# ScalarE's pieces of a second-layer norm queued two bank reads behind their scales, in a fused scan and Hadamard-FFN kernel

## Chip, cores and metric

One core of a Trainium2 chip runs the whole program. The metric is the device time in microseconds (us); lower is better. Float32 throughout.

## What is computed

The input x has 4 images of 512 rows by 512 channels. Two layers are applied, each as `x = x + layernorm(f(layernorm(x)))`. Cut to what matters:

```python
# layer 1: gated scan                      # layer 2: FFN, width 2048
i, f, g = h @ Wi.T, h @ Wf.T, h @ Wg.T     hidden = silu(h @ W1.T) * (h @ W3.T)
gate = sigmoid(f); v = silu(i)*(1-gate)    hidden = fwht(hidden)
o = scan over rows of (gate, v)            out = hidden @ W2.T
o = rms_norm(o) * gnorm * g * sigmoid(g)
out = o @ Wo
```

The Walsh-Hadamard transform (fwht) is folded into W2 once, early in the program.

## The kernel before, in words

**Products.** Every matrix product is split in the Winograd way into seven products of half-size blocks, P1, P2, P6, P5, P7, P3, P4 in this order (`ORDER`, L33; `seven`, L444). A set of seven uses three PSUM banks, X, Y and Z. X takes P1, P6, P7 and P4 one after the other, Y takes P2, Z takes P5 and P3. After each product the bank is read: P1, P6, P5 and P4 are copied out by ScalarE (L470), P2, P7 and P3 are added to a quarter of the result by VectorE (L468). The next product into the same bank has to wait for that read: P6 waits for the copy of P1, P4 for the read of P7. In these texts a "read" means one of the three VectorE reads.

**Units.** An attention unit `attn_unit(b, u)` (L511) is one set for image b: u=0 and u=1 give two halves of the scan, u=2 the output gate. `ffn_unit(b, m)` (L621) is one of eight sets of the first FFN matrices. `attn_out(b)` (L572) is the set for Wo, `ffn_out` (L637) one for W2; these are not run in one go, but put into the queue `fill`. `run` (L112) goes through the seven products k = 0..6 of a unit, and after each of them may take one step from `fill` (`slot`), so the sets of two stages alternate on TensorE. Units (1,0), (1,1), (2,0) and (2,1) are "dense": a slot after every product. The tile names in the profile are X_a, Y_a, Z_a for attention units, X_y, Y_y, Z_y for Wo, X_f for W1 and W3, X_po for W2.

**Small work.** The norm behind Wo and the norm in front of the FFN are cut in pieces that wait in two queues:
- `sums`: VectorE pieces. At each read of a set, `pace[what]` of them are taken (L473-L476): statistics of a quarter, `half` (two row tiles' mean and root), two `residual`s, and `scales` (L606), which issues statistics, a power on GpSimd (`rs`, L244) and the bias `nb` (L274) of the second layer's norm for two of the four row tiles.
- `acts`: ScalarE pieces. After product k of a unit, `pieces[k]` of them are taken (L117-L119), each ordered behind the latest copy of a bank (`behind("copy")`). Dense units take one after k = 0, 2, 3, 5, 6, others one after k = 0 and two after k = 3. The pieces of `scales` are the writes of `xn_f` (L289), which need `nb`. Behind the second piece of a pair follows GpSimd's store of the pair to DRAM, `xnd_f` (L298).

**Fold.** The FFN's input is the transpose of `xn_f`. `load_fold` (L401) reads it back from DRAM with eight DMAs on SyncE's queue, four for each half of the rows; `transpose_fold` (L423) has two steps of four VectorE transposes, one for each half, and a step of four block sums (T1 to T4, L152-L155). The first halves feed the FFN's first two products, the sums the third. For image 0 the load stands in `fold_beside` (L936), which `beside` calls after product k = 2 of unit (2,1). The transposes stand behind reads of units (2,1) and (2,2) (`transpose_beside`, L905). Right behind this load on SyncE's queue stand the first FFN weights, `load_ffn_w(0, 0)` (L943).

**Order.** TensorE and SyncE run in program order. For VectorE, ScalarE and GpSimd a planner orders the instructions when the program is built, by priority (program order, less an offset: 400 for bank reads, `URGENT`) and by its own estimate of when each is ready, and keeps the `behind` edges. On the chip every engine goes through its own list in that order.

The image whose second norm is made beside unit (2,0) is image 0; the Wo set in `fill` at that time belongs to image 1.

Of the kernel before, what the change touches and what calls it, by code (L numbers as in the profile page):

```python
# [44 lines left out]
def kernel(  # L45
# [42 lines left out]
    def bank(name):  # L88
        return psum.tile([P, 2, H], F32, tag="ps", name=name)
# [11 lines left out]

    beside = {}
    acts = deque()
    sums = deque()
    pace = {}
    FULL, SLOW, NONE = (
# [59 lines left out]
    def again(key, b, pool=stream):  # L166
        t = stream_tile(key, b, pool)
        nc.sync.dma_start(out=t, in_=saved[key])
        return t
# [150 lines left out]
    class OutputNorm:  # L320
# [7 lines left out]
        def quarter(self, i, j, tiles=(0, 1)):  # L328
            for t in tiles:
                nc.vector.bn_stats(  # L330
                    self.st[:, 2 * i + t, j, :], self.y[:, i, t, ts(j, H)]
                )
# [111 lines left out]
    def seven(name, multiply, quarter, done=None, add=False, by_tile=False):  # L444

        ps = {}

        def make(what, a, bb, which, first):
            if first:
                ps[which] = bank(f"{which}_{name}")
            multiply(ps[which], a, bb, first)
            split = by_tile and what == "P4"
            q = {"P1": (0, 0), "P5": (1, 1), "P6": (0, 1), "P2": (0, 0), "P7": (1, 1),
                 "P3": (0, 1), "P4": (1, 0)}[what]  # L460
            to = quarter(*q)
            with tc.high_priority(offset=URGENT):
                if split:
                    for t in range(2):
                        nc.vector.tensor_add(to[:, t], ps[which][:, t], to[:, t])
                        done(*q, t)
                elif what in ("P2", "P7", "P3") or add:
                    read[what] = nc.vector.tensor_add(to, ps[which], to)  # L468
                else:
                    read["copy"] = nc.scalar.copy(to, ps[which])  # L470
            if what in ("P2", "P7", "P3", "P4") and done is not None and not split:
                done(*q)
            if what in ("P2", "P7", "P3") and not by_tile:  # L473
                for _ in range(min(pace[what], len(sums))):
                    with tc.issue_after(read[what].ins):
                        sums.popleft()()  # L476

        return [partial(make, *step) for step in ORDER]

    def project(ws, xt, name, after, dense=False):  # L480
# [91 lines left out]
    def attn_out(b):  # L572

        y = {}  # L580
        w = wo_t[0] if b < 3 else [again(("wo", c), b, stream2) for c in range(2)]

        def multiply(ps, a, bb, first):
            og = ogs[b]
            if not y:
                y[0] = work.tile([P, 2, 2, D], F32, tag="wide", name=f"y_{b}", bufs=3)
            for t in range(2):
                for c in range(2):
                    nc.tensor.matmul(  # L589
                        ps[:, t, :], og[:, a, c, ts(t, P)], w[c][:, bb, :],  # L590
                        start=first and t == 0 and c == 0, stop=c == 1,
                        skip_group_check=True,
                    )

        def done(i, j):
            with tc.high_priority(offset=SOON):
                if (i, j) == (0, 0):
                    y[1] = OutputNorm(b, y[0], ves, "y")
                sums.append(partial(y[1].quarter, i, j))

                def norm(residual, t):
                    sums.append(residual)
                    if t == 0:
                        return

                    def scales():  # L606
                        apply = normalize_tiles(b, "f", 2 * i, 2, True)
                        acts.extend(partial(apply, range(t, t + 1)) for t in range(2))

                    sums.append(scales)  # L610

                if j == 1 - i:
                    sums.append(partial(y[1].half, i, norm))

        steps = seven(f"y_{b}", multiply, lambda i, j: y[0][:, i, :, ts(j, H)], done)
        return steps[:4] + [partial(squares, b)] + steps[4:]
# [255 lines left out]
    with behind("P3"):  # L872
        with tc.high_priority(offset=URGENT):
            combine_weights(2)
        with tc.high_priority(offset=SOON):
            apply = [normalize_tiles(1, "a", i, 2, True) for i in (0, 2)]
# [60 lines left out]
        load_fold(0, "f", "ht")  # L937
        transpose_beside(0, "f", ((6, "P3"), (7, "P2"), (8, "P7")))

    beside.setdefault(2, []).append(fold_beside)  # L940
    pace.update(FULL)
    attn_unit(2, 1, True)
    load_ffn_w(0, 0)  # L943
# [107 lines left out]
```

## Time and profile before

| | |
|---|---|
| median of 3 runs | 819.52 us (818.16 to 820.74) |
| the profiled execution's own time | 819.54 us |
| its span, first to last instruction | 817.4 us |
| around the span | 2.1 us |
| mean granted TensorE clock | 0.994 |
| TensorE busy | 803.8 us, 98% |
| VectorE busy | 492.8 us, 60% |
| ScalarE busy | 265.3 us, 32% |
| GpSimd busy | 67.0 us, 8% |

A timeline row gives the start, the duration, the engine, the line, the operation with output and inputs, how many instructions are merged, and in brackets the idle time ahead of it and what ended that. "PEld" is TensorE's weight load, "SPq" SyncE's DMA issue. A matmul of 256 columns shows 379 ns but follows the one before it every 216 ns, so a product of eight takes 1.73 us.

### The profile page before, as it was taken

The page shows a single profiled execution, that of the slowest core. Times are in us where ns is not written, and L with a number is a line of the kernel's source. Part 1 is how long each engine was busy: PE and PEld are TensorE (multiplying, and loading weights), DVE is VectorE, ACT ScalarE, POOL GpSimd, SP SyncE. Part 2 cuts the span into 40 slices and gives each one's busy share as a digit, 9 for nine tenths or more (in the row PEclk, how much of TensorE's full clock was granted, in tenths as well). Part 3 has the DMA queues.
Part 4 walks back from the last instruction along what each step waited for, and adds up shares of the span by engine and source line. Part 5 has one row for each costly group of instructions (what it writes and reads, how often), then busy time and mean ns, then how long its engine had stood idle before and what let it go on. Part 6 is the DMA issues. An engine that isn't in the chain of part 4 may idle for free.

```text
span 817.4 us, 9848 instructions
## 1 busy us (share of the span) xinstructions
PE 803.8 (98%) x3704; PEld 698.6 (85%) x3704; DVE 492.8 (60%) x1002; ACT 265.3 (32%) x376; POOL 67.0 (8%) x105
## 2 busy tenths in 40 slices
PE   9999998999999999999999999999999999999995
PEld 6778887888888888888888888888888888888884
DVE  6988598799777874454335458635543534544345
ACT  4554645444343122122411223323332111331111
POOL 2120102112111010010100000101000000100000
PEclk9999999999999999999999999999999999999998
DMA  9995355666867873544654354726383442544201
GB/s 327 401 351 219 113 220 183 197 238 209 311 245 285 300 277 145 208 162 164 254 157 191 121 163 157 294 91 226 117 254 130 187 180 91 204 156 188 88 4 51
DMA packets 66415, 160.62 MB, mean 196 GB/s; under 512 B 4800, under 2 KB 40256, under 8 KB 66368
## 3 DMA queue, kind: packets, MB, share of 16 engines
q1 hardware_dynamic: 57168, 115.69, 40.6%
q0 software_dynamic: 8480, 43.00, 13.3%
q10 hardware_dynamic: 720, 1.31, 0.4%
q8 instruction: 29, 0.48, 0.2%
q14 instruction: 18, 0.15, 0.1%
HBM read 115.94 MB, written 44.04 MB: 196 GB/s over the span
## 4 chain that ended last, share of the span: by engine, by line
PE 89%; DVE 6%; DMA 2%; issue 1%; POOL 0%; ACT 0%; POOLq 0%; DVEq 0%; SPq 0%
PE X_f L487 26%; PE X_po L647 13%; PE Z_f L487 13%; PE X_a L487 7%; PE Z_po L647 7%; PE Y_f L487 7%; PE X_y L589 3%; PE Y_po L647 3%; PE Z_a L487 3%; PE Y_a L487 2%; DMA wg<-in_Wg_dram 2%; PE Z_y L589 2%; PE h L744 1%; DVE o L523 1%; PE Y_y L589 1%
## 5 line engine op out<-in xcount | busy, mean ns | idle before, releaser
L487 PE MATMUL X_f<-xt_f,w 128*128 128x256 f32 x1024 | 242.1, 379 | 0.1
L487 PEld LDWEIGHTS X_f<-xt_f,w 128*128 128x128 f32 x1024 | 194.1, 190 | 27.3 <-DVE d_f L468 0.5
L470 ACT COPY d_f<-X_f 128x512 f32<-128x512 f32 x96 | 56.1, 585 | 329.8 <-PE X_f L487 289.5
L647 PE MATMUL X_po<-w,ht 128*128 128x256 f32 x512 | 120.9, 379 | 0.2 <-DVE f L468 0.2
L487 PE MATMUL Z_f<-xt_f,w 128*128 128x256 f32 x512 | 120.9, 379 | 0.0
L647 PEld LDWEIGHTS X_po<-w,ht 128*128 128x128 f32 x512 | 97.2, 190 | 13.8 <-DVE f L468 0.6
L487 PEld LDWEIGHTS Z_f<-xt_f,w 128*128 128x128 f32 x512 | 97.3, 190 | 13.2
L468 DVE TENSOR_TENSOR f<-X_po,f 128x512 f32<-128x512 f32 x51 | 35.1, 688 | 93.9 <-PE X_po L647 93.9
L502 DVE TENSOR_TENSOR ht<-d_f 128x1024 f32<-128x1024 f32 x32 | 39.1, 1222 | 60.2 <-ACT d_f L623 45.4
L647 PE MATMUL Z_po<-w,ht 128*128 128x256 f32 x256 | 60.5, 379 | 0.0
L487 PE MATMUL Y_f<-xt_f,w 128*128 128x256 f32 x256 | 60.5, 379 | 0.0
L647 PEld LDWEIGHTS Z_po<-w,ht 128*128 128x128 f32 x256 | 48.6, 190 | 6.6
L487 PEld LDWEIGHTS Y_f<-xt_f,w 128*128 128x128 f32 x256 | 48.6, 190 | 6.6
L468 DVE TENSOR_TENSOR d_f<-X_f,d_f 128x512 f32<-128x512 f32 x32 | 22.1, 690 | 50.7 <-PE X_f L487 43.0
L244 POOL TENSOR_TENSOR rs_f<-rs_f,power 128x2 f32<-128x2 f32 x16 | 13.4, 840 | 406.4 <-DVE nm_f L345 347.1
L470 ACT COPY d_a<-X_a 128x512 f32<-128x512 f32 x36 | 21.0, 583 | 66.7 <-PE X_a L487 66.5
L623 ACT ACTIVATE d_f<-d_f 128x1024 f32<-128x1024 f32 x32 | 33.8, 1057 | 1.0
L487 PE MATMUL X_a<-xt_a,wi 128*128 128x256 f32 x128 | 33.8, 385 | 0.1
L589 PE MATMUL X_y<-wo,og 128*128 128x256 f32 x128 | 31.7, 392 | 2.2 <-ACT y L470 2.2
L487 PE MATMUL X_a<-xt_a,wf 128*128 128x256 f32 x128 | 32.8, 379 | 0.0
L468 DVE TENSOR_TENSOR d_f<-Z_f,d_f 128x512 f32<-128x512 f32 x32 | 21.9, 685 | 16.7 <-PE Z_f L487 16.7
L468 DVE TENSOR_TENSOR f<-Z_po,f 128x512 f32<-128x512 f32 x28 | 19.3, 688 | 20.2 <-PE Z_po L647 20.2
(161 smaller groups left out, 1017.3 us busy)
## 6 DMA issues: line engine op xcount, KB each, us to landing
w<-s_w SPq DMA_DIRECT2D x72, 896.0 KB, 6.2
s_w<-w POOLq DMA_DIRECT2D x24, 896.0 KB, 6.6
w<-in_W_dram SPq DMA_DIRECT2D x32, 256.0 KB, 5.4
wi<-s_wi SPq DMA_DIRECT2D x6, 896.0 KB, 8.4
wf<-s_wf SPq DMA_DIRECT2D x6, 896.0 KB, 7.9
wg<-s_wg SPq DMA_DIRECT2D x6, 896.0 KB, 5.8
w_h<-w2p POOLq DMA_DIRECT2D x8, 512.0 KB, 5.8
xnd_f<-xn_f POOLq DMA_DIRECT2D x8, 512.0 KB, 4.1
```

What stands on the lines that cost most here:

```text
L244: read["power"] = nc.gpsimd.tensor_tensor(r, r, power_t[:, 0:n], ALU.pow)
L468: read[what] = nc.vector.tensor_add(to, ps[which], to)
L470: read["copy"] = nc.scalar.copy(to, ps[which])
L487: nc.tensor.matmul(ps[:, n, :], w[:, a, c, :], xt[:, bb, c, :], start=first and n == 0 and c == 0, stop=c == 1, skip_group_check=True,)
L502: nc.vector.tensor_mul(to.rearrange("p (t k) f -> p k t f", t=2), a.rearrange("p k (t f) -> p k t f", t=2), b2.rearrange("p k (t f) -> p k ...
L523: nc.vector.tensor_tensor_scan(os_[b][:, u, h, :], gate[:, h, :], v[:, h, :], 0.0, ALU.mult, ALU.add)
L589: nc.tensor.matmul(ps[:, t, :], og[:, a, c, ts(t, P)], w[c][:, bb, :], start=first and t == 0 and c == 0, stop=c == 1, skip_group_check=True,)
L623: nc.scalar.activation(d[:, 0], d[:, 0], AF.Silu)
L647: nc.tensor.matmul(ps[:, t, :], hts[b, m][:, a, ts(t, P)], w[m][:, W2[bb], :], start=first and t == 0 and m == ms[0], stop=m == ms[-1], sk ...
L744: nc.tensor.matmul(p, h_sb, t[:, k, :], start=True, stop=True)
```

## The change

ScalarE's pieces of `scales` go into a new queue `scaled` with a count of 1 in place of `acts`. At each read, pieces with count 0 are moved to `acts`, and then the counts of those that are left go down by one; so a piece is moved at the second read after its `scales`. The load of image 0's fold is called after product k = 4 of unit (2,1) in place of k = 2.

```diff
+    scaled = deque()
...
             if what in ("P2", "P7", "P3") and not by_tile:
+                while scaled and scaled[0][0] == 0:
+                    acts.append(scaled.popleft()[1])
+                for entry in scaled:
+                    entry[0] -= 1
                 for _ in range(min(pace[what], len(sums))):
                     with tc.issue_after(read[what].ins):
                         sums.popleft()()
...
                     def scales():
                         apply = normalize_tiles(b, "f", 2 * i, 2, True)
-                        acts.extend(partial(apply, range(t, t + 1)) for t in range(2))
+                        scaled.extend([1, partial(apply, range(t, t + 1))] for t in range(2))
...
-    beside.setdefault(2, []).append(fold_beside)
+    beside.setdefault(4, []).append(fold_beside)
     pace.update(FULL)
     attn_unit(2, 1, True)
```

## The prediction, made before the change was run

> **What bounds the kernel now.** I read the page's engine shares first, then who TensorE waits for, then the timelines of TensorE, ScalarE and VectorE around the one wait of any size, then the granted clock there.
>
> ```profile
> PE 803.8 (98%) x3704; PEld 698.6 (85%) x3704; DVE 492.8 (60%) x1002; ACT 265.3 (32%) x376; POOL 67.0 (8%) x105
> PE X_y L589 <- ACT y L470: 2.2, 1, 2.2
> ```
>
> TensorE is busy for 98% of the span, and in the waits view its longest wait by far is a single one: a product of the Wo set waits for ScalarE's copy of its bank. Elsewhere I compared the starts of products with 216 ns for each matmul: behind the first 12 us no other place loses more than 0.33 us. So a change to ScalarE's or VectorE's order can gain what this one place costs, and no more. The place, on TensorE and then on ScalarE:
>
> ```profile
> 123.83 1.03 PE L487 MATMUL Z_a<-xt_a,wf 128*128 128x256 f32 x4
> 127.05 3.32 PE L589 MATMUL X_y<-wo,og 128*128 128x256 f32 x8 [2.19 <-ACT y L470]
> 130.16 1.43 PE L487 MATMUL X_a<-xt_a,wi 128*128 128x256 f32 x4
> 131.43 1.03 PE L487 MATMUL X_a<-xt_a,wf 128*128 128x256 f32 x4
> ```
>
> ```profile
> 118.47 1.06 ACT L546 ACTIVATE o<-o 128x1024 f32<-128x1024 f32 x1
> 125.22 1.31 ACT L289 ACTIVATE xn_f<-x,nb_f,rs_f 128x512 f32<-128x512 f32 x1 [5.69 <-DVE nb_f L274]
> 126.44 0.56 ACT L470 COPY y<-X_y 128x512 f32<-128x512 f32 x1
> ```
>
> ScalarE stands idle for 5.69 us at a piece of xn_f whose bias is not there. The copy of X_y behind it had its data since 119.5 (the product began at 117.79), and TensorE's P6 into that bank needs it. The bias is late because VectorE has no gap from 117 to 124.4:
>
> ```profile
> 123.70 0.75 DVE L349 SCALAR_TENSOR_TENSOR x<-y,rs_y,x 128x512 f32<-128x512 f32 x1
> 125.02 0.16 DVE L274 SCALAR_TENSOR_TENSOR nb_f<-mv_f,rs_f 128x2 f32<-128x2 f32 x1 [0.58 <-POOL rs_f L244]
> ```
>
> **What the place costs.** P6 was due at 123.83 + 4 x 0.216 = 124.69 and began at 127.05: 2.36 us. Its eight matmuls took 130.16 - 127.05 = 3.11 us from start to start, not 1.73: 1.38 more. The next four took 1.27, not 0.86: 0.41 more. Sum 4.15 us. The second and third terms are a lowered clock:
>
> ```profile
> 117.00:124.70 7.70, 7.70 (x37) 6.58 (x35) 7.44 (x14) 1.54 (x2) 0.77 (x1) 1.00 0.00 0
> 127.00:130.40 3.40, 3.35 (x9) 2.75 (x10) 3.37 (x6) 1.23 (x1) 2.19 (x3) 0.58 0.50 204
> ```
>
> The granted clock (third from the right) is 1.00 before and 0.58 after the wait. A wait of 2.4 us here thus costs up to 1.8 us of slow matmuls on top.
>
> The Trainium skill ("TensorE: Matmul & The Clock Gate", section "HAM oscillation — how this bites in real kernels") has idle gaps of more than about 3.4 us as what lowers the clock. This gap is shorter and the clock fell, so the row decides; by the page's rule the slow stretch would not be the wait's doing, and 2.36 us would be all there is to gain.
>
> **Part 1, the pieces.** I counted the queues by hand. Image 0's first scales come at P3 of unit (1,2). Before, the first xn_f piece was taken after k = 2 of unit (2,0), ahead of P1 of Wo, and the others after k = 5, k = 6 and k = 0 of unit (2,1). With the change the first pair passes P2 of (2,0) and enters acts at its P7; the pieces are taken after k = 5 and k = 6. The second scales (P3 of (2,0)) are unmoved; that pair enters acts at P7 of Wo and is taken after k = 2 and k = 3 of (2,1). No instruction is added or removed.
>
> At k = 5 the latest copy is that of X_y's P1, so the edge itself puts that copy ahead of the first piece. The copy then runs at about 119.6 to 120.2, and P6 starts when due. Removed: 4.15 us. The piece still waits for nb_f at 125.0 and ends at 126.5; the next copy in the queue, of P6, is ready at 126.4, and no product needs it before Wo's P7, some 8 us later. So the wait stays and nothing hurries behind it: cost 0, covered by 8 us of other products.
>
> **Part 2, VectorE loses slack.** With TensorE 4.15 us earlier, VectorE must do the same work sooner. It is busy for 17.24 of the 20 us from 125 to 145 and then idle 3.25 us until P7 of (2,1) at 149.00, about 6.0 us idle in all; 4.15 of it goes, 1.9 stays. A price against that: GpSimd's power for the second bias may now stand behind the store of the first pair, which comes after k = 6 (about 132.8, against 128.5 before), so that nb_f's second is up to 1.6 us later, and VectorE idles for it. 0.3 us remain. Between 0 and 0.5 us, I take 0. One residual of 0.72 us leaves the stretch before the FFN and a later one takes its load on; up to P7 of the FFN's second unit the count of pieces is as before.
>
> **Part 3, the fold.** No SyncE issue lies between the two places, so its order is unchanged; its time is not. Before:
>
> ```profile
> 138.24 1.34 ACT L289 ACTIVATE xn_f<-x,nb_f,rs_f 128x512 f32<-128x512 f32 x1
> 139.87 0.74 POOL L298 DMA_DIRECT2D xnd_f<-xn_f  x1 [7.07 <-ACT xn_f L289]
> 143.37 2.02 SPq L418 DMA_DIRECT2D fold_f<-xnd_f  x4
> 145.48 1.42 SPq L180 DMA_DIRECT2D w<-in_W_dram  x2
> 151.51 1.21 SPq L180 DMA_DIRECT2D w<-in_W_dram  x2
> ```
>
> The last piece now stands behind the copy of (2,1)'s P5, 145.48 before, so 141.3 to 141.9; the piece ends at 143.2, the store goes out at 143.5, and with its 3.4 us the second half's loads start at 147.0, 3.6 later than before. The last of four is issued at 148.4 and lands 4.8 us later (its row before) at 153.2. The two weight loads behind follow at 149.1; the other pair had waited for a buffer until 151.51 and now goes out at 150.5 (the buffer is free at 147.4), landing after 3.2 to 5.5 us, at 157.2 at worst. The FFN's first product, 164.27 before, is due at 160.1: 2.9 us to spare.
>
> The transposes of that half are tighter:
>
> ```profile
> 156.78 1.41 DVE L436 STREAM_TRANSPOSE xt_f<-fold_f 128x256 f32<-128x256 f32 x4
> 158.12 1.18 DVE L523 TENSOR_TENSOR_SCAN o<-d_a 128x512 f32<-128x512 f32 x1
> 161.09 0.69 DVE L468 TENSOR_TENSOR d_a<-X_a,d_a 128x512 f32<-128x512 f32 x1 [1.79 <-PE X_a L487]
> ```
>
> They would start at 152.6 and wait until 153.2 on VectorE's queue, with a scan and the P7 read of (2,2) behind them. The 1.79 us idle ahead of that read take the 0.6; cost 0. Without that cover each us of a later load goes to the read, and 0.8 us further on to TensorE at P4.
>
> **Sum.** 4.15 removed, 0 added: the profiled execution's 819.54 (span 817.4 and 2.1 around it) becomes 815.4. The median of the runs is 819.52, the same. With 0.5 us of Part 2 it is 815.9; the runs before lie within 1.3 us of their median, so 814.3 to 816.6 for this case.
>
> **Rivals.**
>
> *A smaller wait comes in its place (0.14).* VectorE, with 0.3 to 1.9 us to spare near 145, reads a bank late, or the planner, given other arrivals, puts another piece ahead of a copy. For: P7 of the FFN's first unit already starts late, because a square stands ahead of its copy on ScalarE. Against: from 150 on no wait beyond 0.5 us shows. Price 0.5 to 2.4 us with up to 1.8 of clock: 816.6 to 819.
>
> *The slow clock stays (0.03).* If it did not come from the wait, only 2.36 us go: 817.2. Against: it begins right behind the wait, and the windows around it have 1.00.
>
> *Nothing is gained (0.05).* Another instruction that needs late work is put ahead of the same copy: 819.5. The edge excludes the piece itself.
>
> *Slower: the store of the second pair lands late (0.12).* The eight stores xnd_f landed in 3.2 to 8.4 us, median 4.1. At 8.4 us the loads start at 152.0, the last lands at 158.2, the transposes end at 159.6, the scan at 160.8 and the read at 161.4, while P4 of (2,2) is due at 158.4: 3.0 us of wait and 1.7 of slow clock, 4.7 in all, or 820.1. It begins to cost at a landing of 5.4 us; past 10 us the time is above 822. Against: this pair's own stores took 3.3 and 3.4, the second with VectorE busy for 6.51 of 7 us.
>
> The Trainium skill ("SBUF — State Buffer", the "DVE blocks DMA" trap) says that DMAs issued from GpSimd's queue can be held up by VectorE's work, and gives 620 ns growing to about 3100 ns; that would speak for this rival, but the landing of 3.4 us beside a busy VectorE shows no such growth here.
>
> **Numbers.** Forecast 815.4, chance 0.66. The range 814.3 to 818.9 leaves out the last two rivals' 0.17 and a little at the low end. A difference under 0.3% (2.5 us) can't be told from none here. Faster by more means below 817.1: 0.66, half of the first rival and some of the clock's, 0.75. Slower by more means above 822.0: the worse part of the last rival, with unseen reorderings, 0.09. Same: 0.16.
>
> **What would show it.** Right: no wait of X_y on ScalarE's y in TensorE's waits; the copy of Wo's P1 near 119.6 and an xn_f piece behind it near 125; granted clock 1.00 from 124 to 131; the FFN's first product near 160.1; the second half's fold loads near 147. Wrong: a wait of X_a, X_y or X_f above 0.5 us between 125 and 200, SyncE's fold loads past 148.2, or a slow clock without a wait.

## The result, and the profile after

| | before | after |
|---|---|---|
| median of 5 runs each | 818.16 us (817.44 to 820.74) | 814.73 us (814.56 to 815.22) |
| ratio of after to before | | 0.9948, 95% interval 0.9935 to 0.9961 |
| profiled execution, its time | 819.54 us | 815.02 us |
| its span | 817.4 us | 813.2 us |
| mean granted clock | 0.994 | 0.997 |

The kernel is faster by 0.5%. The two spans differ by 4.2 us: one wait went, with the slow matmuls behind it. The two times differ by 4.5 us, because the time around the span is shorter as well, 1.8 us where it was 2.1. The page's shares, and all of TensorE's waits that are left:

```profile
PE 801.8 (99%) x3704; PEld 698.4 (86%) x3704; DVE 492.6 (61%) x1002; ACT 265.3 (33%) x376; POOL 67.5 (8%) x105
```

```profile
PE warm L825 <- POOL ident masks.py:199: 1.4, 1, 1.4
PE X_po L652 <- DVE f L469: 0.2, 1, 0.2
```

X_y no longer stands in this view. The same place in the timelines of TensorE and of ScalarE:

```profile
123.78 1.03 PE L492 MATMUL Z_a<-xt_a,wf 128*128 128x256 f32 x4
124.64 1.89 PE L594 MATMUL X_y<-wo,og 128*128 128x256 f32 x8
126.37 1.03 PE L492 MATMUL X_a<-xt_a,wi 128*128 128x256 f32 x4
```

```profile
119.66 0.59 ACT L471 COPY y<-X_y 128x512 f32<-128x512 f32 x1 [1.14 <-PE X_y L594]
125.16 1.34 ACT L290 ACTIVATE xn_f<-x,nb_f,rs_f 128x512 f32<-128x512 f32 x1 [4.91 <-DVE nb_f L275]
126.57 0.59 ACT L471 COPY y<-X_y 128x512 f32<-128x512 f32 x1
```

ScalarE still idles for 4.91 us until the bias is there. But the copy of Wo's P1 is now in front of that idle time, and P6 begins 0.86 us after the start of the four matmuls before it (4 x 0.216), with no gap. The granted clock (third from the right) is whole where it had been 0.58:

```profile
127.00:130.40 3.40, 3.40 (x17) 2.99 (x16) 3.40 (x9) 2.26 (x4) 1.46 (x3) 1.00 0.55 124
```

Behind the fold nothing is late. The second half's loads on SyncE's queue, the transposes of that half on VectorE with the read behind them, and the FFN's first product:

```profile
146.52 1.78 SPq L419 DMA_DIRECT2D fold_f<-xnd_f  x4
153.45 1.42 DVE L437 STREAM_TRANSPOSE xt_f<-fold_f 128x256 f32<-128x256 f32 x4
156.89 0.69 DVE L469 TENSOR_TENSOR d_a<-X_a,d_a 128x512 f32<-128x512 f32 x1 [0.63 <-PE X_a L492]
160.07 1.89 PE L492 MATMUL X_f<-xt_f,w 128*128 128x256 f32 x8
```

VectorE is still idle for 0.63 us ahead of the P7 read of unit (2,2), where it had 1.79.

### The profile page after: what moved, and what is told of

It is laid out like the page before. It is cut to its first block, busy times and chain, and to the rows that moved or that the text cites. A ratio compares the mean times of both kernels' runs of the same rounds, so it can differ in the third digit from the quotient of the medians.

```text
span 813.2 us, 9847 instructions
## 1 busy us (share of the span) xinstructions
PE 801.8 (99%) x3704; PEld 698.4 (86%) x3704; DVE 492.6 (61%) x1002; ACT 265.3 (33%) x376; POOL 67.5 (8%) x105
## 4 chain that ended last, share of the span: by engine, by line
PE 92%; DVE 4%; DMA 2%; issue 1%; POOL 0%; ACT 0%; POOLq 0%; DVEq 0%; SPq 0%
PE X_f L492 27%; PE X_po L652 13%; PE Z_f L492 13%; PE X_a L492 8%; PE Z_po L652 7%; PE Y_f L492 7%; PE Z_a L492 4%; PE X_y L594 3%; PE Y_po L652 3%; PE Y_a L492 2%; DMA wg<-in_Wg_dram 2%; PE Z_y L594 2%; PE h L749 1%; PE Y_y L594 1%; PE warm L825 1%
## 5 line engine op out<-in xcount | busy, mean ns | idle before, releaser
L492 PEld LDWEIGHTS X_a<-xt_a,wi 128*128 128x128 f32 x128 | 23.9, 190 | 7.7 <-issue 2.9
```

The costliest lines, as they stand in the source:

```text
L492: nc.tensor.matmul(ps[:, n, :], w[:, a, c, :], xt[:, bb, c, :], start=first and n == 0 and c == 0, stop=c == 1, skip_group_check=True,)
```

## The experiments

The theory: the whole gain is the first piece of image 0's first pair no longer standing ahead of one copy, and its size is the wait plus, in some executions, a stretch of slow clock behind it (granted clock 0.5 in place of 1.00). The rivals: the gain is spread over all pieces; it comes from the fold's place; any delay of the pieces does; the slow clock is not the wait's doing. The ratios are to the kernel before on the same chip.

**1. Which pieces, and is it the fold?** Two kernels, made from the kernel after, each hold back a part of the pieces.

```diff
-                        scaled.extend([1, partial(apply, range(t, t + 1))] for t in range(2))
+                        late = (b, i) == (0, 0)        # the other kernel: != (0, 0)
+                        for t in range(2):
+                            piece = partial(apply, range(t, t + 1))
+                            scaled.append([1, piece]) if late else acts.append(piece)
...
-    beside.setdefault(4, []).append(fold_beside)
+    beside.setdefault(2, []).append(fold_beside)       # the other kernel: 4
```

> Only the first pair of pieces of image 0 is held back two reads; all others enter acts at once and the fold's load stays at k = 2. Theory: the whole gain is the first pair's, so the time is that of the kernel after, 814.7 (within 1 us), with no wait of X_y and the clock at 1.00 there. Rival, the gain is spread over the 16 pieces or belongs to the fold's later load: about 818 or in between, 816 to 817.5.

Measured: 815.26 us (6 runs, 815.07 to 816.12), ratio 0.9956 (0.9942 to 0.997), no wait of X_y, clock 0.996 or 0.997 in every run.

> The other way round: all pairs but the first are held back two reads, and the fold's load stands at k = 4. Theory: the wait of 2.4 us at P6 of Wo is back and with it the time of the kernel before, 817.4 to 820.7. Rival (spread, or the fold): 814.7 to 816.

Measured: 818.40 us (12 runs, 816.93 to 819.98), ratio 0.9998 (0.9987 to 1.0009), and the wait is there:

```profile
PE X_y L594 <- ACT y L471: 2.2, 1, 2.2
```

So one pair of eight carries the gain. The other seven, and the fold's later load, are worth nothing that these runs can tell; the load only had to follow the second pair's store, and with the first pair alone it can stay where it was.

**2. Is any delay enough?** One read in place of two:

```diff
-                        scaled.extend([1, partial(apply, range(t, t + 1))] for t in range(2))
+                        scaled.extend([0, partial(apply, range(t, t + 1))] for t in range(2))
```

> All pairs held back one read in place of two, the load at k = 4. The first piece then enters behind the copy of P5 of unit (2,0), one product ahead of the copy of Wo's P1. Theory: what counts is the edge to that copy, which is not there, so the planner puts the piece ahead of it again: the wait of 2.4 us is back, 817.4 to 820.7. Rival: any delay of the pieces brings the gain: 814.7 to 816.

Measured: 818.37 us (12 runs, 816.79 to 821.03), ratio 0.9994 (0.9982 to 1.0006). ScalarE's timeline has the old order, the piece and then the copy:

```profile
125.42 1.31 ACT L290 ACTIVATE xn_f<-x,nb_f,rs_f 128x512 f32<-128x512 f32 x1 [6.64 <-DVE nb_f L275]
126.63 0.57 ACT L471 COPY y<-X_y 128x512 f32<-128x512 f32 x1
```

The delay as such does nothing: without an edge to the copy of Wo's P1 the planner still puts the piece first. That it takes the bias to be ready earlier than it is would explain this; no run shows the planner's estimates. Two reads is the least count that brings the edge.

**3. Is it the late bias?** The kernel before, its queues untouched, with the first scales' steps put ahead on VectorE:

```diff
-                        apply = normalize_tiles(b, "f", 2 * i, 2, True)
+                        with tc.high_priority(offset=URGENT if (b, i) == (0, 0) else 0):
+                            apply = normalize_tiles(b, "f", 2 * i, 2, True)
```

> The kernel before, with only the VectorE and GpSimd steps of image 0's first scales put ahead by priority (400), so that the bias is there near 118 and not at 125; no queue is changed. Theory: the wait came from the late bias alone; the copy of Wo's P1 then runs by 121.7, P6 starts when due, and the time is that of the kernel after, 814.7 to 815.7, unless the statistics now make a block sum or the gate late (up to 0.5 us). Rival: the place of the pieces in the queue costs by itself, or VectorE's steps in front push the gate's products back so far that TensorE waits for them: 817 to 820.

Measured: 815.33 us (6 runs, 814.85 to 816.47), ratio 0.9955 (0.994 to 0.9971). The bias on VectorE, the piece and the copy on ScalarE:

```profile
118.33 0.16 DVE L274 SCALAR_TENSOR_TENSOR nb_f<-mv_f,rs_f 128x2 f32<-128x2 f32 x1 [0.58 <-POOL rs_f L244]
118.53 1.36 ACT L289 ACTIVATE xn_f<-x,nb_f,rs_f 128x512 f32<-128x512 f32 x1 [1.08 <-DVE nb_f L274]
121.20 0.58 ACT L470 COPY y<-X_y 128x512 f32<-128x512 f32 x1
```

The piece is still ahead of the copy, and harmless, because ScalarE waits 1.08 us and not 5.69. So there are two cures of the same value: bring the late input forward, or put the waiting piece behind what is urgent. Both together:

> The kernel after with the early bias of the run with the early bias added. Theory: there is nothing left to gain at this place, so it is the same as the kernel after within 0.5 us. Rival: the bias, early, lets ScalarE run its pieces sooner and the store with them, which gives 0.5 us or more.

Measured: 815.21 us (6 runs), beside 815.14 for the kernel after in the same session (ratios 0.996 and 0.9959). Nothing more is to be had here, and no kernel tried is clearly better than the one after.

**4. Does the slow clock come from the wait?** First both kernels again, run by run.

> The kernel before, unchanged, timed run by run with its granted clock. Theory: the wait of 2.36 us at P6 of Wo is in every run, and the slow clock behind it costs between 0 and 1.8 us (or twice that) by how the wait falls in the clock's own rhythm; then the times spread over 817.2 to 821 and go with the mean granted clock, about 0.002 of clock for each 1.7 us, while the kernel after, without a wait, stays within 0.7 us. Rival: the spread of the kernel before comes from DMA or from start-up; then the clock is the same in its fast and its slow runs.

Measured: 818.17 us (12 runs), ratio to the other runs of the same kernel 0.9992 (0.998 to 1.0005). The eight runs with a mean clock of 0.996 took 817.05 to 818.71, the four with 0.994 took 819.04 to 820.81. In the sessions of the experiments the kernel before ran 84 times: 39 runs at 0.996 or above with a median of 817.75, 45 below with 819.51; over all 84 it is 819.0. The profile of this run is one without a slow stretch, at the same wait:

```profile
127.93 1.99 PE L589 MATMUL X_y<-wo,og 128*128 128x256 f32 x8 [2.19 <-ACT y L470]
129.76 1.03 PE L487 MATMUL X_a<-xt_a,wi 128*128 128x256 f32 x4
```

The eight matmuls took 1.83 us from start to start here, and 3.11 in the profile of before.

> The kernel after, unchanged, beside the kernel before on one chip. Theory: no run has a slow window (0.996 to 0.997 in all), and the median is 814.7 to 815.4; the kernel before has one in about half of its runs (41 of 73 so far), near 819.5 with and 817.8 without. Rival: the kernel after has the two kinds of runs as well, and its first five runs only missed the slower kind.

Measured: 815.14 us (6 runs, 814.6 to 815.79), ratio 0.9959 (0.9944 to 0.9974). All eleven runs of the kernel after are at 0.996 or 0.997.

Then waits of other lengths, made in the kernel after by small instructions that only occupy ScalarE. They copy a table, which nothing reads any more, onto itself.

```diff
+                elif name == "y_1" and what == "P1":
+                    with behind("copy"):
+                        for _ in range(29):            # 39, 20 and 23 in the others
+                            last = nc.scalar.activation(h_sb, h_sb, AF.Identity)
+                    with tc.issue_after(last.ins):
+                        read["copy"] = nc.scalar.copy(to, ps[which])
```

> The kernel after, with 29 small ScalarE instructions (128x128, about 0.23 us each) put ahead of the copy of Wo's P1, so that P6 waits about 1.2 us (0.5 to 2). Theory: the clock falls only when more than about 2 us of idle time lie in one of its 3.4 us windows; a wait of 1.2 us then costs itself alone, the clock stays at 0.996 to 0.997 in every run, and the time is 815.9 (815.2 to 816.7). Rival: any wait lowers the clock in some of the runs: then some of them show 0.994 or 0.995 and 817.6.

> The same with 39 such instructions, for a wait of about 3.4 us (2.7 to 4.2). Theory: nearly every run (some 85%) then has a slow window, so the median is 814.7 + 3.4 + 1.7 = 819.8 (818.5 to 821.5) with the granted clock at 0.994 to 0.995. Rival: the slow clock comes by chance whatever the length of the wait; then no more of the runs than of the kernel before, about half, show it, and the median is nearer to 818.

Both were sized wrong: one instruction took 0.34 us and not 0.23, so the waits were 4.2 and 7.6 us. On ScalarE and on TensorE, with 29 of them:

```profile
119.08 9.87 ACT L473 ACTIVATE had<-had 128x128 f32<-128x128 f32 x29
129.48 3.78 PE L600 MATMUL X_y<-wo,og 128*128 128x256 f32 x8 [4.01 <-ACT y L475]
```

Measured: 822.04 (6 runs) with clocks of 0.992 to 0.994, and 824.54 (6 runs) with 0.990 to 0.993: a slow stretch in every run. With the right size:

> The kernel after with 20 small ScalarE instructions ahead of the copy of Wo's P1; one took 0.34 us in the two probes before, so P6 waits about 1.3 us (20 x 0.34 - 5.5). Theory (the clock falls when about 2 us or more of one 3.4 us window are idle): no run with a slow window, 0.996 to 0.997 throughout, and 814.7 + 1.3 = 816.0 (815.4 to 816.8). Rival: any wait may lower the clock; then some runs show 0.994 or 0.995 and 817.7.

Measured: 816.77 (7 runs, 815.69 to 817.35), all at 0.996 or 0.997; the wait was 1.1 us. That is 0.9 us more than 814.73 + 1.1. In the profiled run P1 of Wo already begins at 118.42, not at 117.74 as in the kernel after, and another wait stands ahead of it, at 58.69:

```profile
PE X_a L498 <- DVE d_a L469: 0.8, 1, 0.8
```

This early wait comes and goes with the same program: the first profile of the kernel before has none, the second one of 0.4 us.

> The same with 23, so that P6 waits about 2.4 us, as in the kernel before, but with the norm's pieces where the change puts them. Theory: this alone gives the time of the kernel before back, 817.2 in the runs without a slow window and 818.9 in those with one, each some half of the runs (27 of 42 had one in the kernel before). Rival: part of the difference comes from the norm's order elsewhere; then 815.5 to 816.5.

Measured: 817.83 (12 runs), ratio 0.9984 (0.9975 to 0.9993); the wait was 2.1 us. Four runs at 0.993 or 0.994 took 818.27 to 818.78, the other eight (one at 0.995, the rest at 0.996 or above) 816.72 to 818.37. So a bare wait at this place, with the norm's pieces where the change puts them, brings back both kinds of runs. Their medians, 816.96 and 818.6, lie 0.8 to 0.9 below those of the kernel before over all sessions (817.75 and 819.51); 0.24 of that is the shorter wait and 0.35 the time around the span (1.77 us here, 2.12 there). The rest, some 0.2 to 0.3, is not explained and too small for these medians to show: against the kernel before in the same session (818.4 and 819.3) the medians lie 1.5 and 0.7 below.

The profiles add up more closely than the medians. From the start of P1 of Wo to the end of the span, less the wait at P6, it is 695.5 us in the kernel after and 695.6 in each of the four full-clock profiles with a wait there (20 and 23 small instructions, second profile of before, all pairs but the first).

Where the trace's record of the clock has a slow stretch, it is 3.41 us long or a multiple of it (3.41 before, 6.83 and 10.24 in the two long waits), and its edges fit a grid of 3.41 us that runs from the first change of clock on. Here is the one of before, by windows of that length:

```profile
124.14:127.55 3.41, 1.22 (x6) 0.76 (x5) 2.79 (x6) 2.33 (x3) 1.12 (x2) 1.00 0.00 0
127.55:130.96 3.41, 3.41 (x9) 2.72 (x9) 3.41 (x8) 1.23 (x2) 1.92 (x3) 0.50 0.66 271
130.96:134.37 3.41, 3.41 (x17) 2.98 (x16) 2.02 (x7) 1.87 (x4) 1.01 (x1) 1.00 1.00 326
```

Laying this grid over each profiled wait, counted from the time at which the product was due, gives the part of it that falls into its fullest window of 3.41 us, up to the first slow one (the late store is experiment 5):

| kernel | wait, us | idle in the fullest window, us | next window |
|---|---|---|---|
| 20 small instructions | 1.10 | 1.10 | full clock |
| kernel before, second profile | 2.36 | 1.35 | full clock |
| late store | 2.47 | 1.53 | full clock |
| 23 small instructions | 2.12 | 1.78 | full clock |
| all pairs but the first | 2.36 | 1.94 | full clock |
| 39 small instructions, first window | 7.6 | 2.20 | half |
| kernel before, first profile | 2.36 | 2.36 | half |
| one read | 2.37 | 2.37 | half |
| 29 small instructions | 4.17 | 3.41 | half |

So in these nine profiles the wait lowers the clock where more than some 2 us of it (between 1.94 and 2.20) fall into one window. A wait of 2.36 us does so or not by where it meets the grid. The ends of the profiles, where TensorE stops for good, are a second test: in six of the fourteen traces the window in which it stops had 1.02 to 1.90 us idle and was followed by full clock, in eight it had 2.48 us or more idle and was followed by half.

Less is needed to keep a slow clock slow. With 29 small instructions the first slow window had only 0.69 us of idle time, and the next was slow too; in all four traces with a slow stretch the clock came back behind the first slow window without idle time.

The Trainium skill ("TensorE: Matmul & The Clock Gate", section "What's actually happening") has such a window, 3413 ns long and not reset when a kernel starts. The traces agree on both: their windows are 3.41 us long, and the first change of clock comes anywhere from 4.4 to 7.5 us into the span, while the first matmul is at 1.36 or 1.37 us in all fourteen. The rule of the Trainium skill (same page, section "HAM oscillation — how this bites in real kernels"), gaps of more than about 3.4 us, is too lenient for this case by the table.

**5. What if the second store is late?** The last piece of the second pair and the load moved behind the copy of P4 of (2,1):

```diff
+                            if (b, i, t) == (0, 1, 1):
+                                held_back.append(piece)
+                            else:
+                                scaled.append([1, piece])
...
     def fold_beside():
+        with behind("copy"):
+            held_back.pop()()
         load_fold(0, "f", "ht")
         transpose_beside(0, "f", ((6, "P3"), (7, "P2"), (8, "P7")))
+        for other in beside.pop(6):
+            other()
-    beside.setdefault(4, []).append(fold_beside)
+    beside.setdefault(6, []).append(fold_beside)
```

> The kernel after, but the last piece of image 0's second pair is taken only after k = 6 of unit (2,1), behind the copy of P4, and the fold's load with it. By the steps of the prediction: the piece ends near 150.0, the store goes out at 150.3 and lands after 3.1 to 4.8 us, the loads of the second half start at 153.4 to 155, the transposes wait at the head of VectorE's queue until 156 to 159.6, and the P7 read of (2,2) behind them is done at 160 to 162.8, while P4 is due at 158.4: a wait of X_a on VectorE of 1.5 to 4.5 us, and 816.5 to 821. Rival: the transposes are covered by other work however late they come; then 814.7 to 815.5.

Measured: 816.03 us (8 runs, 815.12 to 818.42), ratio 0.9967 (0.9953 to 0.998). The loads came when expected (153.36), but no X_a waits. On SyncE's queue, on TensorE and on VectorE:

```profile
155.24 2.58 SPq L182 DMA_DIRECT2D w<-in_W_dram  x4
163.47 1.13 PE L493 MATMUL X_f<-xt_f,w 128*128 128x256 f32 x4 [2.31 <-DMA w<-in_W_dram]
156.95 0.69 DVE L470 TENSOR_TENSOR d_a<-X_a,d_a 128x512 f32<-128x512 f32 x1 [0.63 <-PE X_a L493]
159.27 1.42 DVE L438 STREAM_TRANSPOSE xt_f<-fold_f 128x256 f32<-128x256 f32 x4
```

The planner saw the later load and put the transposes behind the read. What became late were the first FFN weights, queued behind the fold's loads: the second matrix landed at about 163.4, and the product that needed it was due at 161.0. The price was 1.0 us in the median, 0.3 of it around the span, and 2.4 us of span in the profiled run: less than expected and by another way.

## Why the prediction was right in its mechanism, and which step failed

**The place and its cure: right.** All rests on the copy of Wo's P1: forecast at 119.6, it ran at 119.66, the piece at 125.16 (125.0), the FFN's first product at 160.07 (160.1). Experiments 1 to 3 show that this one order is the whole effect inside the span.

**The price of the place: right for the profile, not for every run.** The sum had 2.36 us of wait and 1.79 of slow clock, 4.15; the spans differ by 4.2. The rival that the slow clock stays is refuted by experiment 4. But the 1.79 is paid in about half of the executions, so the gain has two values. The 11 runs of the kernel after have a median of 815.0; the two kinds of runs of before lie 2.7 and 4.5 us above it, and all 84 together 4.0. By their spans (medians 815.6 and 817.4, and 813.2 after) it is 2.4 and 4.2, the two sums without and with the slow clock.

**The step that failed: "The median of the runs is 819.52, the same", and the scatter of 1.3 us put around the result.** This step takes 4.15 us, the price of a run with the slow clock, from a median as if every run paid it, and carries the scatter over as noise. Two kinds of runs lay in that scatter, and that the median of three was one of the slower kind was luck; two more runs moved it to 818.16. The kernel after has one kind and runs within 0.7 us of itself in its first session. The measured 814.73 lies inside the range, near its low end; the ratio applied to the five-run median of before, 0.9948 x 818.16 = 813.9, lies 0.4 below it. The step should have taken each kind by itself: 817.75 - 2.36 and 819.51 - 4.15 both give 815.4.

**A second term of that sum was mis-sized: "2.1 around it".** The time around the span was carried over as it was. It is 2.06 to 2.18 us in all 84 runs of before and 1.72 to 1.82 in all 11 of after. These 0.3 us are most of what separates the forecast 815.4 from the 815.02 of the profiled execution; the span itself was forecast to 0.1 us. Why they went is open: the time is 2.1 us with the first pair alone and 1.8 in the kernel before with the early bias, so it goes neither with the wait nor with the queue.

**VectorE's slack: right at 0, one term was not there.** The power for the second bias was to stand behind the first pair's store until 132.8. The planner put the piece ahead of the gate's steps on ScalarE that I had in front of it, the store went out at 130.40 and the power at 131.25, and the second bias came at 132.80 as before (132.83).

**The fold: right at 0, with one landing far off.** The second half's loads were forecast for 147.0 and came at 146.52, its store having landed in 3.1 us. But the first pair's store took 8.7 us, where it had taken 3.3; its loads started at 139.16. So a landing as late as the slower rival's did come, but at the store for which nothing waits (its transposes ran at 148). Of GpSimd's queue and SyncE's, around that store:

```profile
127.83 1.46 POOL L768 DMA_DIRECT2D w_h<-w2p  x2 [2.90 <-DVE w2p L764]
130.40 0.73 POOL L299 DMA_DIRECT2D xnd_f<-xn_f  x1 [1.11 <-ACT xn_f L290]
127.43 0.32 SPq L169 DMA_DIRECT2D wg<-s_wg  x1
```

Two stores of 512 KB stand right ahead of it, and the gate's weights of 896 KB, whose buffer TensorE frees 4.2 us earlier than before, are under way at the same time. Other profiles suggest that it takes both. In the first profile of before three such stores within 2 us, with the gate's load 2.4 us behind the last, landed in 3.1 to 4.0 us; in the second the load went out 0.7 us behind the last one, and that one took 7.8. With 23 small instructions only two such stores stood there, with the load 0.6 us behind the second, and they landed in 3.1 and 4.3. No run was made for this alone, so it stays an argument.

**The slower rival's path: wrong.** It had the transposes at the head of VectorE's queue as what breaks first, from a landing of 5.4 us on. Experiment 5 shows that the planner moves them, and that the weights behind the loads give way first.

## What to carry to other kernels

An instruction that waits at the head of an in-order queue costs what is queued behind it: look at what the next instruction there serves, and give the urgent one an edge ahead of the late one, or bring the late input forward; either was worth all there was. A delay that gave no such edge was worth nothing here. When a short TensorE wait goes, price it with and without the slow clock, and read the granted clock run by run before taking a median as the base.

## What the runs showed of the hardware that I had not expected

- A TensorE wait of 2.1 to 2.4 us is followed by half the clock for 3.41 us in some executions and not in others, by how much of it falls into one window of 3.41 us: 1.94 us did not, 2.20 did. A wait of 1.1 us never did in 7 runs. In a window that is already slow, 0.69 us of idle time was enough to keep the next one slow.
- A ScalarE instruction of 128x128 that writes what it reads took 0.34 us in a row of 20 to 39, each waiting for the one before, where I had estimated 0.23 from 128x256 rows of 0.42.
- The same kind of store (512 KB to DRAM on GpSimd's queue) landed in 3.1 to 8.7 us within one profile.
